# Neighbour weights in PSUM, key-query products on GpSimd, sums on VectorE, and key monomials over three chunks

## The chip, the core and the metric

The kernel runs on one core of a Trainium2 chip. The core has a matrix engine (TensorE, PE in the profile, with its weight loads shown as PEld), a vector engine (VectorE, DVE), a scalar engine (ScalarE, ACT), a general engine (GpSimd, POOL) and a queue engine that mostly starts transfers (SyncE, SP). Each works through its own instructions in order and waits for the others through semaphores. Data lies in SBUF (128 partitions) or in PSUM, where TensorE writes its results. The metric is the device time of one execution in microseconds.

## The reference

Four graph layers act on a table x of 2708 nodes by 128 features, with one 2708 x 2708 matrix `adj` of which some 0.15% of the entries, and the diagonal, differ from zero:

```python
h = relu(layernorm(x)); x = x + laplacian(adj) @ (h @ W + b)             # layer 0
h = relu(layernorm(x)); x = x + attention(h)                             # layer 1
h = relu(layernorm(x)); x = x + relu(batchnorm(adj.T @ h / deg ...))     # layer 2
h = relu(layernorm(x)); x = x + gated_sum(h, adj)                        # layer 3

# layer 1: d = 128 groups of 8 values, n = 2708
q = (x @ Wq.T).reshape(d, n, 8);  k, v alike
a = softmax(einsum('dnh,dmh->dnm', q, k) * d ** -0.5 + 2 * adj, axis=2)
out = einsum('dnm,dmh->dnh', a, v).reshape(n, 8 * d) @ Wo.T
```

Layer 1 takes most of the time. It is 128 attentions over all 2708 nodes, with 8 values per query and key.

## The kernel before

**How layer 1 is computed.** The kernel never forms the 2708 x 2708 logits. With no adjacency term, exp(q.k) is replaced by a polynomial in the 8 values of q and k, so that the sum over all keys becomes a small matrix of moments. The adjacency term is then put in exactly, for those pairs only where `adj` isn't zero (the neighbours), by adding exp(q.k)(exp(2 adj) - 1) times the value. The two parts are summed and divided by the summed weight (the ninth column of the values).

**The loop over d.** For each of the 128 d's, the 2708 nodes are 22 tiles of up to 128 rows, in six chunks of at most four tiles. The pieces of one d are:

- `keys(d)`: GpSimd makes the monomials of the keys (`bk` and `fk`, 12 products, all recorded at line 1010 as `mul_g` is the recording line). `with_values` makes `y`, low monomials times values, on GpSimd as well, in two halves.
- `moments`: TensorE multiplies `fk` by `y` and sums into `m_ps` (line 1048). `weighted` scales that into `mw` on VectorE (line 1058).
- `queries(d)`: VectorE makes the monomials of the queries (`fq`, line 1007).
- `turn(d, c)`: TensorE transposes `fq` of one chunk into `f_ps` (line 1074), and ScalarE copies it to `fT` (line 1076).
- `evaluate(d, c)`: TensorE multiplies `fT` by `mw` into `g_ps` (line 1086). VectorE multiplies by the low monomials (`z`, line 1094) and sums (`o_raw`, line 1100).

The loop is written out by hand, in what is called a manual schedule, so the order of the calls in the program is the order in each engine's queue. In each chunk it issues `keys(d + 2)` if the chunk is the first, `weighted` if it is the last, `evaluate(d, c)`, three steps of `queries(d + 1)`, `turn` for the next chunk, some of the `moments(d + 1)`, one half of `with_values(d + 2)` in the third and the last chunk, and one step of `prepare`, which loads the q, k and v of a later group of four d's.

**The work beside the loop.** After these calls every chunk takes PACE = 1.45 steps of a generator `first`, which is in turn: a search of `adj` for the neighbours together with gathers by node (`search`, `by_node`), then sorting the nodes by their number of neighbours (`in_order`), then `from_neighbours`. When it is used up, the chunk instead takes up to three steps of a second list, `beside`: `normalise(g)` for each of 32 groups of d's and `project_out` for each of 22 row tiles. What is left of `beside` is stepped through after the loop.

**`from_neighbours`.** The sorted nodes lie in 22 tiles with room for 16, 9, 8, ... 2 neighbours each (`ROOM`), 121 neighbour slots in all. For each slot b, GpSimd's queue loads the keys and values of the neighbours by an indirect transfer (`c_kv`, line 825, 1.05 MB). Then `logits(b)` multiplies keys by queries (`c_z`, line 840, VectorE), yields a step and sums over the 8 values (`c_c`, line 844, VectorE). `weigh(b)` takes the exponential and scales it on ScalarE. `values(b - 1)`, which is called between the two, first copies the previous slot's weights to the ninth column of `c_v` on ScalarE, then multiplies values by weights (line 870, VectorE), yields twice, and adds the product to the tile's sum `c_acc` (line 879, GpSimd). The first slot of a tile writes its product to `c_acc` directly, so 99 of the 121 have a sum. When a tile is finished, its sum is scattered to `more_n`. The weights `c_c` are tiles of 128 x 128 in SBUF, from a rotating pool.

**`normalise` and `project_out`.** `normalise(g)` loads the group's `o_raw` and `more_n`, adds them on GpSimd (`r_raw`, line 930), and on VectorE takes the reciprocal (`r_rs`, line 932) and the product (`r_on`), which is stored. `project_out(t)` loads a row tile and multiplies it by Wo (`l_o`, line 505, TensorE, into the pool `ps_t` of two buffers that `turn` also uses), and VectorE adds the result to `x_sb` (line 508).

**After the loop.** A guard reduces bounds of the data to two counts in `flag`, `once` and `heads`. Three loops over these counts recompute attention in full where the polynomial would not be accurate enough; for this data the counts are zero, and the loops are skipped. Then layer 2 loads its weights, takes `norm_relu`, makes 1/deg and spreads it over the partitions through 22 small products (`d_ps` into `diB`), and multiplies `h` by `adj` (`pg`), for which each tile of `adj` is loaded into `a2` from a pool of four buffers. Layer 3 follows.

Of the kernel before, what the change touches and what calls it, by code (L numbers as in the profile page):

```python
# [16 lines left out]
P = 128  # L17
BK = 512
# [31 lines left out]
def gnn4_kernel(  # L50
# [75 lines left out]
    few = keep.tile([P, 1], FP, name="few")  # L126

# [388 lines left out]
    with ExitStack() as ph:  # L516
# [8 lines left out]
        ps_t = ph.enter_context(tc.tile_pool(name="l1_pst", bufs=2, space=PSUM))  # L525
        ps_m = ph.enter_context(tc.tile_pool(name="l1_psm", bufs=1, space=PSUM))
        ps_g = ph.enter_context(tc.tile_pool(name="l1_psg", bufs=2, space=PSUM))
        ps_q = ph.enter_context(tc.tile_pool(name="l1_psq", bufs=1, space=PSUM))

# [272 lines left out]
        def from_neighbours():  # L802
# [6 lines left out]
            qs, kvs, cs, accs = {}, {}, {}, {}  # L809
            done = []  # L810
# [23 lines left out]
            def logits(b):  # L834
                t, s0, w = todo[b]
                sz = rows[t][1]
                cs[b] = sm.tile([P, S, C], FP, name="c_c")
                for e in range(w):
                    z = tm.tile([P, C, HEAD], FP, name="c_z", tag="tmp")
                    nc.vector.tensor_tensor(  # L840
                        z[:sz], kvs[b][:sz, e, :, 0], qs[t][:sz], ALU.mult
                    )
                    yield
# [14 lines left out]
            def values(b):  # L858
# [6 lines left out]
                for e in range(w):  # L865
# [11 lines left out]
                    yield  # L877
                    if s0 + e:
                        nc.gpsimd.tensor_tensor(acc[:sz], acc[:sz], z[:sz], ALU.add)  # L879
# [118 lines left out]
        PACE = 1.45  # L998
# [16 lines left out]
        def keys(d):  # L1015

            k = got[d // GRP][0][:, d % GRP, :, k_at]
            fks[d] = fp.tile([P, NT, F_ALL], FP, name="fk")
            run(features(mul_g, k, bks[d % 2], fks[d]))
# [86 lines left out]
        with tc.manual_schedule():  # L1106
# [4 lines left out]
            keys(0)  # L1111
# [3 lines left out]
            keys(1)  # L1115
# [10 lines left out]
            for d in range(D):  # L1126
                asked = queries(d + 1) if d + 1 < D else iter(())
                for c in range(NCH):
                    if d + 2 < D and c == 0:
                        while len(got) <= (d + 2) // GRP:  # L1130
                            run(soon.pop(0))
                        keys(d + 2)
# [29 lines left out]
                if (d + 2) % GRP == 0 and (d + 2) // GRP + 1 < NG:  # L1162
                    soon.append(prepare((d + 2) // GRP + 1, got))
            while beside or under_way:
# [4 lines left out]
    with ExitStack() as ph:  # L1169
        gp = ph.enter_context(tc.tile_pool(name="l1g", bufs=1))  # L1170
        gw = ph.enter_context(tc.tile_pool(name="l1g_w", bufs=2))
        g_l = ph.enter_context(tc.tile_pool(name="l1g_l", bufs=1, space=PSUM))
        g_t = ph.enter_context(tc.tile_pool(name="l1g_t", bufs=1, space=PSUM))
        g_o = ph.enter_context(tc.tile_pool(name="l1g_o", bufs=1, space=PSUM))
        q_f = dram.tile([N, P, HEAD], FP, name="q_f")
        k_f = dram.tile([N, P, HEAD], FP, name="k_f")
        v_f = dram.tile([N, P, VW], FP, name="v_f")
        o_f = dram.tile([N, P, HEAD], FP, name="o_f")

        nc.vector.memset(top, 0.0)
        p2 = gp.tile([C, 2], FP, name="p2")
        for e in range(2):
            pt = g_t.tile([P, BK], FP, name="g_tr", tag="tr")
            nc.tensor.transpose(pt[:C, :P], most2[:, e], ident)
# [414 lines left out]
```

## Time and profile before

| What | Value |
|---|---|
| Time, median of 3 runs | 4456.89 us (4449.6 to 4462.39) |
| The profiled execution's own time | 4452.14 us |
| Its span in the trace | 4450.3 us |
| Busy: PE, DVE, ACT, POOL | 3230.9, 3549.0, 1101.9, 2789.4 us |
| First `z` to last `o_raw` of the loop | 470.2 us to 3921 us |
| First to last neighbour product `c_z` | 1318.7 us to 3300.7 us |
| TensorE clock granted, mean | 0.842 |

The span runs from the first to the last record of the core, and the device time is about 2 us more. A group's row gives line, engine, operation, output and inputs, shape and count, then the busy time in us and the mean of one in ns, then the idle time of the engine just ahead of these instructions and what ended most of it. A tile's row gives the minimum, median and maximum of one in ns, and when the first began and the last ended. Busy time of an engine that waits inside an instruction[...] counts as busy.

### The profile page before, as it was taken

Reading aid. Unit: us, or ns where it says so; the run is one execution under the profiler, and the core shown is the slowest. Engines: PE = TensorE matmul, PEld = TensorE weight load, DVE = VectorE, ACT = ScalarE, POOL = GpSimd, SP = SyncE. Lnnn points to the kernel's source line nnn. Section 1 sums busy time; section 2 is a strip of 40 time slices with the busy share of each in tenths; the row PEclk is TensorE's granted clock in tenths of the full one; section 3 lists DMA queues with packets and bytes.
Section 4 is the critical chain, followed back from the end, with each engine's and each line's share of the span. In section 5 each row is a group of like instructions: output and inputs, shape, how many; then the busy total and the mean of one; then the engine's idle time right before and its main releaser. Section 6 shows DMA issues by size and latency. Waiting matters only on the chain. (4 is left out here: it accounts for less than half of the span.)

```text
span 4450.3 us, 49671 instructions
## 1 busy us (share of the span) xinstructions
PE 3230.9 (73%) x17298; PEld 2879.4 (65%) x17298; DVE 3549.0 (80%) x4852; ACT 1101.9 (25%) x2497; POOL 2789.4 (63%) x2384
## 2 busy tenths in 40 slices
PE   7986788888857777776777766767767788949434
PEld 5953677788756666666666656667657787834223
DVE  5988899987849989999988999999977777840322
ACT  4246233333312222222222222222221111210110
POOL 0001766677767887887878777678876666700266
PEclk9988889899978888888888888888888899979565
DMA  4637344367412222222222222222324454035232
GB/s 181 225 143 304 101 108 123 98 140 178 110 54 80 84 79 90 90 91 81 90 90 91 81 76 96 82 94 97 104 70 105 112 113 96 23 103 203 75 86 70
DMA packets 402006, 480.25 MB, mean 108 GB/s; under 512 B 290672, under 2 KB 322098, under 8 KB 376916
## 3 DMA queue, kind: packets, MB, share of 16 engines
q1 hardware_dynamic: 370140, 308.03, 24.1%
q0 software_dynamic: 31600, 168.86, 11.5%
q8 instruction: 144, 2.36, 0.2%
q14 instruction: 122, 1.00, 0.1%
HBM read 363.13 MB, written 113.67 MB: 107 GB/s over the span
## 5 line engine op out<-in xcount | busy, mean ns | idle before, releaser
L1086 PE MATMUL g_ps<-mw,fT 128*128 128x189 f32 x5632 | 1227.8, 366 | 699.1 <-DVE mw L1058 397.8
L1086 PEld LDWEIGHTS g_ps<-mw,fT 128*128 128x128 f32 x5632 | 1043.2, 215 | 781.0 <-issue 521.9
L1010 POOL TENSOR_TENSOR y<-bk,raw 128x2079 f32<-128x2079 f32 x256 | 976.2, 3814 | 516.1 <-PE m_ps L1048 478.3
L1048 PE MATMUL m_ps<-y,fk 128*128 128x189 f32 (+1 forms) x5632 | 1101.7, 340 | 21.3 <-POOL y L1010 21.3
L1048 PEld LDWEIGHTS m_ps<-y,fk 128*128 128x128 f32 (+1 forms) x5632 | 963.5, 203 | 50.5 <-issue 28.7
L1076 ACT COPY fT<-f_ps 128x512 f32<-128x512 f32 (+1 forms) x768 | 422.7, 550 | 1962.1 <-PE f_ps L1074 1960.1
L1094 DVE TENSOR_TENSOR z<-g_ps,bq 128x756 f32<-128x756 f32 (+1 forms) x768 | 669.4, 872 | 202.4 <-PE g_ps L1086 201.7
L1100 DVE TENSOR_REDUCE o_raw<-z 128x36 f32<-128x756 f32 (+1 forms) x768 | 672.5, 876 | 26.3
L1074 PE MATMUL f_ps<-ident,fq 128*128 128x128 f32 x2816 | 490.3, 299 | 38.9 <-DVE fq L1007 36.2
L1010 POOL TENSOR_TENSOR fk<-bk,raw 128x528 f32<-128x528 f32 (+1 forms) x512 | 508.2, 1021 | 0.0
L1074 PEld LDWEIGHTS f_ps<-ident,fq 128*128 128x128 f32 x2816 | 400.5, 157 | 75.7 <-issue 31.5
L840 DVE TENSOR_TENSOR c_z<-c_kv,c_q 128x1024 f32<-128x1024 f32 (+1 forms) x121 | 419.5, 3467 | 10.6 <-DMA c_kv<-kv_n,srt 10.6
L879 POOL TENSOR_TENSOR c_acc<-c_acc,c_v 128x1152 f32<-128x1152 f32 (+1 forms) x99 | 262.1, 2647 | 165.6 <-DVE c_v L870 119.1
L1010 POOL TENSOR_TENSOR fk<-raw,bk 128x352 f32<-128x352 f32 (+1 forms) x512 | 317.7, 649 | 0.0
L1007 DVE TENSOR_TENSOR fq<-bq,q_ps 128x528 f32<-128x528 f32 (+1 forms) x512 | 288.0, 604 | 0.0
L870 DVE TENSOR_TENSOR c_v<-c_kv,c_c 128x1024 f32<-128x1024 f32 (+1 forms) x99 | 244.5, 2470 | 1.3 <-POOL c_acc L879 1.3
L465 POOL MEMSET qkv<- 128x512 f32 x6 | 6.3, 1083 | 374.8 <-PE l_o L350 255.4
L1010 POOL TENSOR_TENSOR bk<-raw 128x88 f32<-128x88 f32 (+1 forms) x512 | 216.7, 454 | 33.4 <-DMA raw<-qkv_c 32.9
L1420 POOL DMA_INDIRECT g<-gate_d,srt x121 | 122.6, 1013 | 107.7 <-issue 107.7
L825 POOL DMA_INDIRECT c_kv<-kv_n,srt x121 | 137.3, 1135 | 60.2 <-DVE c_acc L870 37.5
L1007 DVE TENSOR_TENSOR fq<-q_ps,bq 128x352 f32<-128x352 f32 (+1 forms) x512 | 171.7, 377 | 0.0
L505 PE MATMUL l_o<-woT,o_cr 128*128 128x128 f32 (+1 forms) x352 | 95.8, 421 | 81.2 <-DMA o_cr<-o_c 40.2
(284 smaller groups left out, 3502.7 us busy)
## 6 DMA issues: line engine op xcount, KB each, us to landing
a_nat<-in_adj_dram SPq DMA_DIRECT2D x32, 1354.0 KB
qkv_c<-qkv SPq DMA_DIRECT2D x5, 6400.0 KB
a<-in_adj_dram SPq DMA_DIRECT2D x21, 1354.0 KB
kv_n<-n_kv SPq DMA_DIRECT2D x32, 672.0 KB
an<-in_adj_dram SPq DMA_DIRECT2D x15, 1354.0 KB
o_g<-o_raw SPq DMA_DIRECT2D x32, 396.0 KB
r_raw<-o_g SPq DMA_DIRECT2D x32, 396.0 KB
r_more<-more_n SPq DMA_DIRECT2D x32, 396.0 KB
```

The lines of the kernel that those rows point to most:

```text
L825: nc.gpsimd.indirect_dma_start(out=kvs[b][:sz, e].rearrange("p c e k -> p (c e k)"), out_offset=None, in_=kv_n.rearrange("n c k -> n (c k) ...
L840: nc.vector.tensor_tensor(z[:sz], kvs[b][:sz, e, :, 0], qs[t][:sz], ALU.mult)
L870: nc.vector.tensor_tensor(z[:sz, :, :HEAD], kv[:sz, e, :, 1], c[:sz, e, :, None].to_broadcast([sz, C, HEAD]), ALU.mult,)
L879: nc.gpsimd.tensor_tensor(acc[:sz], acc[:sz], z[:sz], ALU.add)
L1007: nc.vector.tensor_tensor(o, x, y, ALU.mult)
L1010: nc.gpsimd.tensor_tensor(o, x, y, ALU.mult)
L1048: nc.tensor.matmul(pms[d][:, : B_ALL * VW], fks[d][:sz, t], ys[d, h][:sz, m].rearrange("p k b -> p (k b)"), start=t == 0, stop=t == NT - 1,)
L1074: nc.tensor.transpose(pt[:, m], fqs[d][:, t0 + m], ident)
L1076: nc.scalar.copy(fts[d, c][:, :n], pt[:, :n])
L1086: nc.tensor.matmul(pg[:, m, : B_ALL * VW], ft[:, m], mws[d].rearrange("p k b -> p (k b)"), start=True, stop=True,)
L1094: nc.vector.tensor_tensor(z[:, :n], pg[:, :n, : B_ALL * VW].rearrange("p t (k b) -> p t k b", k=VW), bqs[d % 2][:, t0 : t0 + n, None, :B_A ...
L1100: nc.vector.reduce_sum(ros[g][:, t0 : t0 + n, i], z[:, :n], axis=AX.X,)
```

## The change

1. `logits`: the product `c_z` of keys and queries is issued on GpSimd, and there are two yields instead of one ahead of its reduction on VectorE.
2. The weights `c_c` are no longer SBUF tiles. Two slots alternate in one PSUM tile, `c_two`, from a new pool `ps_c` of one bank. To make room, `ps_t` has one buffer where it had two.
3. `values`: the sum into `c_acc` is issued on VectorE, one yield after `c_v`. A first slot now has one yield and the others two; before, every slot had two.
4. PACE is 1.58 instead of 1.45.
5. `keys(d + 2)` is a generator. Five of its products are issued in the first chunk, five in the second and the last two in the third.
6. The guard stands ahead of the leftover steps of `beside`, takes its buffers from the loop's pools, and `flag` is kept in a longer-lived pool.
7. Layer 2's weights, biases, `diB` and the loads of the first four `adj` tiles stand ahead of the three loops of the fallback, which moved inside layer 2. `norm_relu` stays after them.

```diff
-        ps_t = ph.enter_context(tc.tile_pool(name="l1_pst", bufs=2, space=PSUM))
+        ps_t = ph.enter_context(tc.tile_pool(name="l1_pst", bufs=1, space=PSUM))
...
+        ps_c = ph.enter_context(tc.tile_pool(name="l1_psc", bufs=1, space=PSUM))
...
+            c_two = ps_c.tile([P, 2, S, C], FP, name="c_c")
...
-                cs[b] = sm.tile([P, S, C], FP, name="c_c")
+                cs[b] = c_two[:, b % 2]
                 for e in range(w):
                     z = tm.tile([P, C, HEAD], FP, name="c_z", tag="tmp")
-                    nc.vector.tensor_tensor(
+                    nc.gpsimd.tensor_tensor(
                         z[:sz], kvs[b][:sz, e, :, 0], qs[t][:sz], ALU.mult
                     )
+                    yield
                     yield
                     nc.vector.reduce_sum(cs[b][:sz, e], z[:sz], axis=AX.X)
...
                     yield
-                    yield
                     if s0 + e:
-                        nc.gpsimd.tensor_tensor(acc[:sz], acc[:sz], z[:sz], ALU.add)
+                        nc.vector.tensor_tensor(acc[:sz], acc[:sz], z[:sz], ALU.add)
+                        yield
...
-        PACE = 1.45
+        PACE = 1.58
...
-            run(features(mul_g, k, bks[d % 2], fks[d]))
+            yield from features(mul_g, k, bks[d % 2], fks[d])
...
-                        keys(d + 2)
+                        keyed = keys(d + 2)
+                    if d + 2 < D:
+                        for _ in range(5 if c < 2 else NCH * 3):
+                            next(keyed, None)
...
+            nc.vector.memset(top, 0.0)
+            p2 = sm.tile([C, 2], FP, name="p2")
...
             while beside or under_way:
                 if not step(n, NG):
                     n += 1
-        nc.vector.memset(top, 0.0)
-        p2 = gp.tile([C, 2], FP, name="p2")
...
+        with tc.tile_pool(name="l2_ps0", bufs=2, space=PSUM) as ps:
+            wnT = transposed(lp, wk_pool, ps, wn2, "wnT")
...
+            for t, (r0, sz) in enumerate(rows):
+                dg = lp.tile([P, P], FP, name="dg", tag="dg", bufs=2)
+                nc.vector.tensor_scalar_mul(dg[:sz, :sz], ident[:sz, :sz], di[:sz, t : t + 1])
+                pd = ps.tile([P, BK], FP, name="d_ps", tag="tr")
+                nc.tensor.matmul(pd[:, :sz], ones[:sz], dg[:sz, :sz], start=True, stop=True)
+                nc.scalar.copy(diB[:, r0 : r0 + sz], pd[:, :sz])
+        for t in range(min(4, NT)):
+            rows_of_adj2(t)
```

## The prediction

> **What bounds the kernel now.** I read the page first, then busy time by stage, then the tiles of the neighbour code, then a timeline. The page has the engines' busy time and the groups that the change touches.
>
> ```profile
> PE 3230.9 (73%) x17298; PEld 2879.4 (65%) x17298; DVE 3549.0 (80%) x4852; ACT 1101.9 (25%) x2497; POOL 2789.4 (63%) x2384
> ...
> L840 DVE TENSOR_TENSOR c_z<-c_kv,c_q 128x1024 f32<-128x1024 f32 (+1 forms) x121 | 419.5, 3467 | 10.6 <-DMA c_kv<-kv_n,srt 10.6
> L879 POOL TENSOR_TENSOR c_acc<-c_acc,c_v 128x1152 f32<-128x1152 f32 (+1 forms) x99 | 262.1, 2647 | 165.6 <-DVE c_v L870 119.1
> ...
> L870 DVE TENSOR_TENSOR c_v<-c_kv,c_c 128x1024 f32<-128x1024 f32 (+1 forms) x99 | 244.5, 2470 | 1.3 <-POOL c_acc L879 1.3
> ```
>
> No engine is full over the span, so I cut it into stages by the tiles' first and last times: the search, the gathers by node, the sorting in order, the neighbours, the normalisation, the rest of the loop, the tail, layers 2 and 3. Columns after window and length: busy PE, weight load, DVE, ACT, POOL; clock; DMA share; GB/s.
>
> ```profile
> 470.00:910.00 440.00, 349.44 (x1993) 327.02 (x1991) 419.24 (x558) 140.17 (x263) 287.20 (x268) 0.88 0.41 104
> 910.00:1210.00 300.00, 271.38 (x1659) 254.80 (x1660) 244.53 (x413) 116.36 (x227) 227.04 (x206) 0.97 0.65 151
> ...
> 1318.00:3305.00 1987.00, 1410.41 (x7605) 1321.85 (x7606) 1871.96 (x2180) 453.86 (x1149) 1576.43 (x1229) 0.84 0.26 87
> 3305.00:3770.00 465.00, 371.76 (x2028) 351.31 (x2027) 340.22 (x549) 79.97 (x187) 315.21 (x264) 0.88 0.46 105
> 3770.00:3921.00 151.00, 137.05 (x849) 128.67 (x847) 123.21 (x203) 34.42 (x77) 94.75 (x83) 0.98 0.10 24
> ```
>
> The neighbours' 1987 us are 45% of the span, and VectorE is busy for 1872 of them (94%), GpSimd for 79%, PE for 71%. So VectorE sets the pace there. Yet its neighbour products take longer than they need (minimum/median/maximum ns):
>
> ```profile
> L840 DVE TENSOR_TENSOR c_z<-c_kv,c_q x121: 1215/3453/14609, 1318.7 to 3300.7; 128x1024 f32<-128x1024 f32 x119, 20x1024 f32<-20x1024 f32 x2
> L870 DVE TENSOR_TENSOR c_v<-c_kv,c_c x99: 1212/1653/8760, 1343.7 to 3322.6; 128x1024 f32<-128x1024 f32 x98, 20x1024 f32<-20x1024 f32 x1
> L844 DVE TENSOR_REDUCE c_c<-c_z x121: 1197/1210/1223, 1322.2 to 3305.5; 128x128 f32<-128x1024 f32 x119, 20x128 f32<-20x1024 f32 x2
> L1094 DVE TENSOR_TENSOR z<-g_ps,bq x768: 725/932/969, 470.2 to 3920.6; 128x756 f32<-128x756 f32 x128, 128x567 f32<-128x567 f32 x64
> ```
>
> Both products read two SBUF operands and range widely; the reduction (one operand) and z (one operand in PSUM) don't. The timeline (start, duration) shows why:
>
> ```profile
> 1668.04 3.78 POOL L1010 TENSOR_TENSOR y<-bk,raw 128x2079 f32<-128x2079 f32 x1
> 1669.19 3.72 DVE L840 TENSOR_TENSOR c_z<-c_kv,c_q 128x1024 f32<-128x1024 f32 x1
> 1673.02 1.22 DVE L844 TENSOR_REDUCE c_c<-c_z 128x128 f32<-128x1024 f32 x1
> ```
>
> c_z ends 1.1 us after y does (1671.82), that is, one undisturbed product later: it had stood behind GpSimd's instruction.
>
> [...]
>
> **The change, part by part.** The loop has 768 chunks, each with one z. The built order says how many lie before the first neighbour's reduction, between the first and the last, and after: 213/412/143 before, 196/441/131 after. A neighbour takes more steps (704 in all against 605), so there are .274 per chunk instead of .294.
>
> Neighbour stage, VectorE per chunk. Before, 1872 less the neighbours' own instructions (419.5 + 121×1.21 + 244.5 + 47.0 for the 21 first-neighbour products = 857.5) is 1014 over 412 chunks, 2.46 us, unchanged. After, per neighbour: c_z 0 here; reduction 1.21; c_v 1.22, because its weight comes from PSUM and it no longer contends (saving 1.25 on 99 of them); the sum c_acc, now on VectorE with two SBUF inputs, in .818 of the neighbours (99/121): 1.36 if free, up to 3.9 if it waits as c_z did (c_z's mean wait of 2.25 plus 1.36 is 3.6). Taken 3.3, since GpSimd is about as busy as before. Bank waits: in the built order 40 of 121 reductions stand directly ahead of the previous neighbour's c_v, while ScalarE's weight copy stands between them; I take 0.55 us for the copy and hand-offs, .18 per neighbour (0 to .3). Lateness of GpSimd: .3 per neighbour (0 to 2.5). Sum 1.21+1.22+.818×3.3+.18+.3 = 5.61; ×.274 = 1.54. With 2.46 and the .28 of other idle per chunk as before ((1987-1872)/412), 4.28 us per chunk, ×441 = 1887: **-100**. Ends: 3.96 per chunk (1746, -241), where the sum hardly waits (VectorE then needs 3.7) and GpSimd, below, is the next bound; and 4.45 (1962, -25) with the sum at 3.9 and the bank at .3, the mishap R3 apart.
>
> GpSimd per chunk. Before, 1576.4 - 262.1 (sums) - 137.3 (loads' issue) = 1177/412 = 2.86. After, 2.86 + .274×(1.14 + 2.4 for c_z, 1024×2.3 ns) = 3.83, which is 89% of 4.28. So it is the second bound, close behind. PE's moment products wait for its y, and the c_kv loads are issued from its queue.
>
> Where the product moves, GpSimd's queue matters. A c_z may stand behind a y (3.8 us) or key monomials (12 products, 8.5 us, in one block before; now 5, 5 and 2). Its reduction is programmed two steps later, 2/1.58 chunks × 4.28 = 5.4 us. If it is late, everything of VectorE stands behind the reduction, z too, and then PE with both g_ps buffers full. In the trace GpSimd runs ahead: the sums start a median 0.14 us, mean 2.3, and in one of ten 8.3 after their c_v, though they are programmed some 6.6 us later; lateness beyond 5.4 us is then rare, hence .3.
>
> Fewer chunks ahead: the search ends at chunk 99 instead of 107; VectorE, 95% busy there, saves 8×2.46 = 20. The gathers save 8 chunks at PE's 3.3 (its cycle is 18 to 20 us per six chunks): 26. Sorting, which waits for DMA, and the same work in fewer chunks: +2. Together **-44**.
>
> Fewer chunks after: 12×2.6 (between VectorE's 2.46 and PE's 3.2) = **-31**; the normalisations themselves take the same number of steps.
>
> ps_t from two buffers to one (its place goes to the weights): a transpose then waits for ScalarE's 0.55 us copy of the one before, and l_o for VectorE's x_sb add. It is hidden while VectorE bounds (PE is 71% busy), but not in 3305 to 3921, where PE is 80 to 91%: **+30** (0 to 60).
>
> Key monomials spread: y's products no longer wait for 8.5 us of monomials, worth something in the PE-bound stages, -20 (0 to -40); but normalisation's r_raw products move later in GpSimd's queue, +10 (VectorE's r_rs waits 34.8 us for r_raw there now). **-10**.
>
> Tail: the guard (4.5 us of VectorE) goes ahead of the last normalisation, which waits for r_more's landing: -4.5, hidden there. One loop skip (about 3 us of 9.3) comes while the tail still works: -3. The 22 small products for diB move ahead of the skips, serial over three engines: +12, less 5 to 9 of PE in layer 2 where they lay before; the adjacency loads start sooner, but layer 2's product is PE-bound (4.54 us per tile), so this earns nothing. **+2** (-8 to +15).
>
> Sum: -100 -44 -31 +30 -10 +2 = -153. The profiled run took 4452.1 (span 4450.3, 2 us around it), so 4299; the median of the runs shown is 4.8 higher, so **4305**.
>
> **Rivals.** R1, the port wait nearly vanishes. The sum now follows c_v on VectorE and may meet short GpSimd monomials rather than y; at 3.96 us per chunk a further -141: 4165. Against it: GpSimd's busy share hardly falls. Chance .17. R2, GpSimd becomes the bound: busy 3.83 plus the waits it keeps (y for PE's m_ps, 131 us in this stage now, .32 per chunk; c_z for the landing or for buffers) gives 4.4 to 4.6 per chunk, 4350 to 4440. For it: 89% leaves little room. Chance .17. R3, slower: c_z reaches the front of GpSimd's queue too late and VectorE stands at the reduction. From 4305, a mean extra wait w costs 121×w; from w = 1.25 us it cancels the gain, and at 2.5 (half a y and some monomials each time) the time is 4305 + 300 = 4605, less what the wait takes from the sum's port wait, some 60: 4545. Against it: GpSimd runs ahead now, and it gives up 262 us of sums for 290 of products (2.4×121) that are spread over 29 more chunks. Chance .08. R4, the weight in PSUM does not free c_v: +1.25×99 = 124, so 4430. Against it: z's tight durations. Chance .04.
>
> **How the numbers follow.** Likeliest .54, 4235 to 4365 by its own terms. Runs of this kernel differ by about 0.3% (13 us), so the border of faster is 4444. R1 and R2's lower part are inside 4195 to 4420, which leaves out R3, R4 and the far tails, about .2. Faster: .54 + .17 + .15 + .02 = .88; same: .02 + .01 = .03 from R2 and R4; slower: R3 and some of R4, .09.
>
> **What would show it.** Right: in the neighbour stage about 4.3 us per chunk, c_v tight at 1.22 to 1.25 us, c_acc on VectorE 3 us in the mean and as wide as c_z was, c_z on GpSimd 2.3 to 2.5, GpSimd near 89%, little wait of the reduction for c_z (under 40 us in all), a ScalarE wait around c_c of some 20 us; the stage begins some 44 us sooner. Wrong: waits of the reduction for GpSimd of over 100 us (R3); waits on y or c_kv that grow while VectorE falls under 85% (R2); c_acc under 2 us (R1); c_v still over 1.6 us (R4); PE waits for ScalarE's copy beyond 60 us after the stage (ps_t).

## The result, and the profile after

The changed kernel takes 4428.92 us in the median (14 runs, 4415.62 to 4445.41), the kernel before 4455.6 us beside it (14 runs). The ratio is 0.9944, with a 95% interval from 0.9922 to 0.9966. So it is faster by 25 us (0.6%), about one sixth of the 150 that were forecast, and it lies above the range of 4195 to 4420. The profiled execution has a span of 4420.4 us, 30 less than the one of before.

The stages show where the forecast was lost. Lengths are taken between the same instructions in both traces: the loop's first z, the first c_z, the end of the last reduction into c_c, the loop's last z, the end.

| Stage | Before, us (chunks) | After, us (chunks) | Difference | Forecast |
|---|---|---|---|---|
| Search, gathers, sorting | 848 (213) | 817 (196) | -31 | -44 |
| Neighbours | 1988 (412) | 1984 (441) | -4 | -100 |
| Rest of the loop | 614 (143) | 614 (131) | 0 | -11 |
| From the last z to the end | 530 | 536 | +6 | +2 |

Such lengths vary by themselves. The changed kernel and seven of the kernels below have the same code, at PACE 1.58, from the neighbours to the last z; the rest of the loop takes 614 to 637 us in them. The run with the old tail, which has the changed kernel's neighbour code, takes 1993 us for that stage instead of 1984.

The page of the changed kernel, with busy time and share per engine, and then the groups that were moved (busy us, mean ns, idle time ahead):

```profile
PE 3259.3 (74%) x17298; PEld 2894.7 (65%) x17298; DVE 3374.6 (76%) x4830; ACT 1092.1 (25%) x2497; POOL 2792.6 (63%) x2406
...
L882 DVE TENSOR_TENSOR c_acc<-c_acc,c_v 128x1152 f32<-128x1152 f32 (+1 forms) x99 | 379.5, 3834 | 1.4
...
L843 POOL TENSOR_TENSOR c_z<-c_kv,c_q 128x1024 f32<-128x1024 f32 (+1 forms) x121 | 285.9, 2363 | 2.1 <-DMA c_kv<-kv_n,srt 0.7
```

VectorE lost 174 us of busy time (3549.0 to 3374.6), GpSimd kept its own (2789.4 to 2792.6). Yet the span fell by 30 only. The same by stage, for the neighbours and the rest of the loop (columns as before: window, length, then busy PE, weight load, DVE, ACT, POOL):

```profile
1287.00:3271.00 1984.00, 1479.80 (x8138) 1390.04 (x8139) 1770.68 (x2285) 467.61 (x1206) 1662.27 (x1333) 0.86 0.26 89
3271.00:3885.00 614.00, 492.28 (x2647) 458.77 (x2645) 424.26 (x690) 103.90 (x240) 372.92 (x307) 0.88 0.36 84
```

In the neighbour stage VectorE is busy for 1771 us (1872 before) and idle for 213 (115 before). So of its work 101 us went, although 29 more chunks lie in the stage, and 98 us came back as idle time. The tiles tell which work remained (minimum/median/maximum ns):

```profile
L843 POOL TENSOR_TENSOR c_z<-c_kv,c_q x121: 2307/2341/3452, 1287.2 to 3255.9; 128x1024 f32<-128x1024 f32 x119, 20x1024 f32<-20x1024 f32 x2
L874 DVE TENSOR_TENSOR c_v<-c_kv,c_c x99: 1195/1216/1223, 1315.2 to 3275.3; 128x1024 f32<-128x1024 f32 x98, 20x1024 f32<-20x1024 f32 x1
L882 DVE TENSOR_TENSOR c_acc<-c_acc,c_v x99: 1347/2754/12153, 1318.2 to 3276.6; 128x1152 f32<-128x1152 f32 x98, 20x1152 f32<-20x1152 f32 x1
```

c_v, with its weight in PSUM, is now as tight as z was: every one takes 1.2 us. The sum has inherited the wide spread of c_z: 1.35 us where it is free, 12.2 at worst, 3.83 in the mean. VectorE's waits in the neighbour stage tell where it stood idle: the instruction, what it waited for, us in all, times, longest. The two longest before the change, and then those after it:

```profile
DVE c_acc L870 <- DMA more_n<-c_acc,srt: 47.5, 11, 12.2
DVE z L1094 <- PE g_ps L1086: 44.1, 47, 1.8
```

```profile
DVE z L1098 <- PE g_ps L1090: 82.4, 75, 3.3
DVE c_acc L874 <- ACT c_acc L873: 65.5, 19, 9.3
DVE c_c L848 <- POOL c_z L843: 34.2, 23, 5.9
DVE c_v L874 <- ACT c_v L873: 15.5, 32, 0.8
```

The line of c_acc after the change is put down to ScalarE's copy into a fresh c_acc; that copy itself had waited for the scatter of the tile before (105.9 us in all, 17 times). Ahead of the reduction and of c_v, VectorE's idle time before the change was 3 and 1 us.

What a long sum is waiting for shows in the timeline of one that took 9.0 us (start, duration; GpSimd, then VectorE):

```profile
1384.70 3.83 POOL L1014 TENSOR_TENSOR fk<-bk,raw 128x528 f32<-128x528 f32 x4
1388.51 3.75 POOL L1014 TENSOR_TENSOR y<-bk,raw 128x2079 f32<-128x2079 f32 x1
1392.41 1.91 POOL L828 DMA_INDIRECT c_kv<-kv_n,srt  x1 [0.16 <-issue]
...
1384.48 9.00 DVE L882 TENSOR_TENSOR c_acc<-c_acc,c_v 128x1152 f32<-128x1152 f32 x1
```

The forecast had read c_z's wait as one for the GpSimd instruction in progress. This sum waited longer than that: through four more key products and a y, which follow one another without a gap, and ran when GpSimd paused by 0.16 us ahead of a load.

### The profile page after: what moved, and what is told of

Its sections match the earlier page's. It is cut to its first block, busy times and chain, and to the rows that moved or that the text cites. A ratio compares the mean times of both kernels' runs of the same rounds, so it can differ in the third digit from the quotient of the medians.

```text
span 4420.4 us, 49434 instructions
## 1 busy us (share of the span) xinstructions
PE 3259.3 (74%) x17298; PEld 2894.7 (65%) x17298; DVE 3374.6 (76%) x4830; ACT 1092.1 (25%) x2497; POOL 2792.6 (63%) x2406
## 5 line engine op out<-in xcount | busy, mean ns | idle before, releaser
L1052 PE MATMUL m_ps<-y,fk 128*128 128x189 f32 (+1 forms) x5632 | 1118.5, 344 | 34.6 <-POOL y L1014 34.6
L1052 PEld LDWEIGHTS m_ps<-y,fk 128*128 128x128 f32 (+1 forms) x5632 | 977.9, 206 | 64.2 <-POOL y L1014 35.3
L882 DVE TENSOR_TENSOR c_acc<-c_acc,c_v 128x1152 f32<-128x1152 f32 (+1 forms) x99 | 379.5, 3834 | 1.4
L843 POOL TENSOR_TENSOR c_z<-c_kv,c_q 128x1024 f32<-128x1024 f32 (+1 forms) x121 | 285.9, 2363 | 2.1 <-DMA c_kv<-kv_n,srt 0.7
L828 POOL DMA_INDIRECT c_kv<-kv_n,srt x121 | 167.2, 1382 | 128.2 <-DVE c_v L874 50.8
L1014 POOL TENSOR_TENSOR bk<-raw 128x88 f32<-128x88 f32 (+1 forms) x512 | 195.7, 412 | 33.8 <-DMA raw<-qkv_c 33.5
L848 DVE TENSOR_REDUCE c_c<-c_z 128x128 f32<-128x1024 f32 (+1 forms) x121 | 147.7, 1221 | 34.3 <-POOL c_z L843 34.2
L506 PE MATMUL l_o<-woT,o_cr 128*128 128x128 f32 (+1 forms) x352 | 107.2, 442 | 82.4 <-DVE x_sb L509 56.5
```

Source lines behind the costliest of these rows:

```text
L828: nc.gpsimd.indirect_dma_start(out=kvs[b][:sz, e].rearrange("p c e k -> p (c e k)"), out_offset=None, in_=kv_n.rearrange("n c k -> n (c k) ...
L843: nc.gpsimd.tensor_tensor(z[:sz], kvs[b][:sz, e, :, 0], qs[t][:sz], ALU.mult)
L848: nc.vector.reduce_sum(cs[b][:sz, e], z[:sz], axis=AX.X)
L882: nc.vector.tensor_tensor(acc[:sz], acc[:sz], z[:sz], ALU.add)
L1014: nc.gpsimd.tensor_tensor(o, x, y, ALU.mult)
L1052: nc.tensor.matmul(pms[d][:, : B_ALL * VW], fks[d][:sz, t], ys[d, h][:sz, m].rearrange("p k b -> p (k b)"), start=t == 0, stop=t == NT - 1,)
```

## The experiments

What the forecast and the expectations call the wait for the port is here a group's busy time less its count times what one takes when free (1.216 us for a product, 1.353 for a sum). That a port which VectorE and GpSimd share is behind it was my reading and is not shown. The traces show durations: with both operands in SBUF, c_z took 1215 to 14609 ns before the change and the sum 1347 to 12153 after it; with one of them in PSUM, c_v took 1195 to 1223 beside a GpSimd that was busy for 1662 of the 1984 us. In the neighbour stage before the change these port waits are 419.5 - 121×1.216 = 272 us in c_z, 240.0 - 98×1.216 = 121 in c_v and 21 in the first products, 414 in all; after it, 376.3 - 98×1.353 = 244, all in the sum. Every run below was timed in five rounds against the kernel before; its ratio has an interval of about 0.0025 to each side (11 us) unless one is given. The column "us" compares it with the changed kernel, as (ratio - 0.9944)×4440; such a difference is good to some 15 us.

| Run | Ratio | us | Neighbour stage, us | VectorE busy / idle there | Port waits |
|---|---|---|---|---|---|
| changed kernel | 0.9944 | 0 | 1984 | 1771 / 213 | sum 244 |
| sum with one SBUF input | 0.9808 | -60 | 1906 | 1699 / 207 | product 231 |
| sum with one input in PSUM | 0.9438 | -225 | 1757 | 1517 / 240 | none |
| engines swapped back | 1.0062 | +52 | 2005 | 1824 / 181 | c_z 287 |
| weights in SBUF, one ps_t | 1.0176 | +103 | 2088 | 1884 / 204 | c_v 171, sum 183 |
| weights in SBUF, two ps_t | 1.0081 | +61 | 2112 | 1938 / 174 | c_v 199, sum 206 |
| keys in one block | 1.0091 | +65 | 2015 | 1742 / 273 | sum 213 |
| PACE 1.45 | 0.9785 | -71 | 2040 (480 chunks) | 1815 / 225 | sum 190 |
| copy ahead of the reduction | 0.9843 | -45 | 1933 | 1737 / 196 | sum 213 |

**Is VectorE still the bound?** Two edits of the sum, each of one instruction, and each leaves the earlier neighbours out:

```diff
-                        nc.vector.tensor_tensor(acc[:sz], acc[:sz], z[:sz], ALU.add)
+                        nc.vector.tensor_scalar_mul(acc[:sz], z[:sz], 1.0)
```

> The changed kernel, with VectorE's sum of c_acc and c_v replaced by a product of c_v with 1.0, so that the instruction reads one SBUF operand; the earlier neighbours' sum is left out of the result. V (VectorE still sets the pace of the neighbour stage, and the sum's wait for the port, (3834 - 1357) x 99 = 245 us, is what ate the gain): the instruction takes 1.4 us at most, the stage loses 200 to 245 us of its 1984, the time falls to 4190 to 4240. P (another engine or wait bounds the stage now, so VectorE's time is no longer worth its length): the time falls by less than 90 us, to 4340 or more, and VectorE's idle time grows by over 150 us.

It gave 4354.78 us, 0.9808. By its time that is P's case, but VectorE's idle time did not grow (207 us): the instruction still waited.

```profile
L882 DVE TENSOR_SCALAR c_acc<-c_v x99: 748/1799/11549, 1315.9 to 3195.4; 128x1152 f32<-128x1152 f32 x98, 20x1152 f32<-20x1152 f32 x1
```

It is fast where it is free (748 ns, where the sum of as many elements takes 1347), and as wide as the sum otherwise; its mean in the stage is 3108 ns, so it waits 2.36 us where the sum waits 2.49. The reduction too reads one SBUF operand, and it doesn't wait inside itself (1197 to 1223 ns before the change). I had counted operands only, and their number does not tell the two apart; what does is not shown. What was saved, 72 us of VectorE's busy time, came off the stage in full (78). The second edit takes operands like those of c_v's own product, which is tight: one in SBUF, one in PSUM (lines joined):

```diff
-                        nc.vector.tensor_tensor(acc[:sz], acc[:sz], z[:sz], ALU.add)
+                        nc.vector.tensor_tensor(
+                            acc[:sz, :, :HEAD], z[:sz, :, :HEAD],
+                            c[:sz, e, :, None].to_broadcast([sz, C, HEAD]), ALU.mult)
```

> The changed kernel with the sum replaced by a product of c_v and the weights in PSUM (1024 elements, one SBUF operand and one in PSUM, as c_v's own product is); the earlier neighbours' sum is left out of the result. This takes away the port's wait that the product with 1.0 had kept (3.1 us in the mean). V (VectorE's length sets the neighbour stage): the instruction takes 1.22 us, the stage loses (3840 - 1220) x 98 = 257 us less what GpSimd, 84% busy, and TensorE give back as new waits, so 150 to 250 us, and the time falls to 0.94 to 0.963 of the kernel before. P (another engine is next at once): the stage loses under 110 us, idle time of VectorE rises above 350 us, 0.97 or more.

It gave 4196.26 us, 0.9438 (0.9413 to 0.9463), at the good end of V. Its tile and its neighbour stage:

```profile
L882 DVE TENSOR_TENSOR c_acc<-c_v,c_c x99: 1204/1215/1224, 1321.4 to 3055.8; 128x1024 f32<-128x1024 f32 x98, 20x1024 f32<-20x1024 f32 x1
...
1290.00:3048.00 1758.00, 1420.28 (x8143) 1335.83 (x8144) 1517.38 (x2285) 465.80 (x1205) 1577.46 (x1331) 0.90 0.30 100
```

VectorE's busy time fell by 254 us, the stage by 227, to 3.98 us per chunk, and there GpSimd is the busiest engine (90%). So at 4.50 us per chunk neither GpSimd nor TensorE was the bound: VectorE's length was, with its waits in place.

**What does the swap earn?** In the changed kernel, with each instruction at its new place:

```diff
-                    nc.gpsimd.tensor_tensor(
+                    nc.vector.tensor_tensor(
                         z[:sz], kvs[b][:sz, e, :, 0], qs[t][:sz], ALU.mult
...
-                        nc.vector.tensor_tensor(acc[:sz], acc[:sz], z[:sz], ALU.add)
+                        nc.gpsimd.tensor_tensor(acc[:sz], acc[:sz], z[:sz], ALU.add)
```

> The changed kernel with both engines swapped back: c_z on VectorE, the sum on GpSimd, each at its new place in the program. Everything else (weights in PSUM, one ps_t buffer, pace, key monomials, tail) stays. S (the swap earns nothing, since the port wait goes with whichever two-SBUF-input instruction VectorE has): c_z 3.3 to 3.6 us on VectorE (+410), the sum's 380 off it, the time within 30 us of the changed kernel, 4400 to 4460. O (the swap is what earned the gain, the weights in PSUM nothing): 4460 or more. H (the swap itself costs, by putting VectorE behind GpSimd at the reduction): 4330 to 4400.

4464.02 us, 1.0062: just at O's number, 52 us slower, though O's reason (the weights earn nothing) does not hold, as the runs on the weights show. In the neighbour stage it costs 21 us only: VectorE is busy 53 longer, 43 of them port waits (287 in c_z for 244 in the sum), and idle 32 less. After it the loop takes 637 us instead of 614, which is within what the same code varies by, so where the rest of the 52 lies is open. VectorE's wait for g_ps is 45 us here and 82 in the changed kernel. It is 44 to 49 in every profiled kernel with c_z on VectorE and 67 to 104 in every one with c_z on GpSimd; why the product's place should make TensorE late is not shown. The same swap alone, on the kernel before (with its yields, PACE 1.45):

> The kernel before with the swap alone: c_z on GpSimd, the sum on VectorE, with the yields of the change, PACE 1.45, weights in SBUF, keys in one block. E (the swap gains by itself, as its undoing says): 0.975 to 0.99. I (without the spread keys c_z comes late, and c_v takes the waits that c_z had): waits of the reduction for c_z over 60 us, c_v's waits over 200 us, 0.995 to 1.02.

4470.56 us, 1.0099 (1.0078 to 1.012): slower by 44, inside theory I's range, with both of its waits a little under the size that it named:

```profile
L871 DVE TENSOR_TENSOR c_v<-c_kv,c_c x99: 1202/1748/11214, 1355.0 to 3527.0; 128x1024 f32<-128x1024 f32 x98, 20x1024 f32<-20x1024 f32 x1
L879 DVE TENSOR_TENSOR c_acc<-c_acc,c_v x99: 1335/2065/11768, 1358.1 to 3529.8; 128x1152 f32<-128x1152 f32 x98, 20x1152 f32<-20x1152 f32 x1
```

Now c_v waits 165 us and the sum 150, and the reduction stands 59 us for c_z. VectorE has two waiting instructions per neighbour, as it had before.

**The PSUM edit.** In the changed kernel, first the weights alone go back (their PSUM pool goes too), then the second ps_t buffer as well:

```diff
-                cs[b] = c_two[:, b % 2]
+                cs[b] = sm.tile([P, S, C], FP, name="c_c")
```

> The changed kernel with the weights c_c back in rotating SBUF tiles, and still one ps_t buffer. W (c_v has to wait for the port again, 1.25 us each in 99, and the bank's waits go): +124 - 16 = about +108 in VectorE's stage, 4500 to 4550. B (the bank's waits cost about as much as the port): 4410 to 4450.

> The same, with two ps_t buffers as before the change, so the whole of the edit on PSUM is undone. Against the run with one buffer: T (the single buffer makes TensorE late, f_ps behind v_sum in the neighbour stage, l_o behind x_sb after it): 50 to 90 us faster, with VectorE's waits for g_ps and l_o back at 44 and 30 us in these stages. N (it only costs in the normalisation stage): 20 to 40 us faster. If it falls below the changed kernel's time, the edit on PSUM as a whole was a loss.

4516.64 us (1.0176) and 4481.16 us (1.0081). The weights in PSUM are worth 103 us, as W said: without them c_v has 171 us of port waits and the sum 61 less. The single ps_t buffer costs 42 by the ratios (35 by the medians), which is N, so the whole edit on PSUM is worth 61. VectorE's waits for g_ps in the neighbour stage are 82 with one buffer and 67 with two, and the stage is no shorter with two (2112 for 2088, in a profiled run 19 us above the median of its runs); after the stage the loop takes 614 us against 585, and x_sb shows where (the groups of the two runs in that stretch, one buffer first; idle time ahead is the last number):

```profile
L509 DVE TENSOR_TENSOR x_sb<-x_sb,l_o 128x128 f32<-128x128 f32 x72 | 20.5, 285 | 62.1 <-PE l_o L506 61.8
```

```profile
L509 DVE TENSOR_TENSOR x_sb<-x_sb,l_o 128x128 f32<-128x128 f32 x72 | 20.5, 284 | 29.5 <-PE l_o L506 28.2
```

The edit alone on the kernel before:

> The kernel before with the edit on PSUM alone: weights c_c in one PSUM tile of two slots, one ps_t buffer. E (the edit pays by itself, as its undoing on the changed kernel says): c_v 1.22 us, VectorE's waits in c_v and first products (142 us) gone, some 42 us lost to the single buffer, 0.975 to 0.987 of the kernel before. I (c_z takes over c_v's waits, since a VectorE that is ahead meets GpSimd sooner, or the bank's order costs as much): c_z's waits rise from 272 to over 350 us, 0.99 to 1.005.

4393.26 us, 0.9921: 35 us faster, less than E. The number is in I's range, but not for I's reason: c_z did not take the waits over, it waited less (234 us for 272). VectorE's idle time took them over:

```profile
DVE c_acc L872 <- ACT c_acc L871: 124.6, 19, 12.6
DVE z L1096 <- PE g_ps L1088: 45.6, 58, 2.1
DVE c_v L872 <- ACT c_v L871: 19.0, 32, 2.1
```

The stage lost 180 us of port waits (414 to 234) and 71 in length, because the wait of a tile's first product for the last tile's scatter went from 48 to 125 us, and 19 us went to the wait of c_v for ScalarE's copy.

**The key products.** With all twelve in the first chunk again:

```diff
-                        for _ in range(5 if c < 2 else NCH * 3):
+                        for _ in range(NCH * 3):
```

> The changed kernel with all twelve key products issued in the first chunk again. L (the spreading makes fk late for the moments or delays c_z and normalisation): faster than the changed kernel by 20 to 50 us, 0.983 to 0.990 of the kernel before. G (it helps c_z reach GpSimd in time): slower by 10 to 50 us, with VectorE's wait for c_z up from 34 us to over 60; 0.997 to 1.006.

> The kernel before with the key products spread over three chunks alone. E (spreading pays by itself, y comes sooner and the runs on GpSimd are shorter): 0.983 to 0.993 of the kernel before. I (it pays only with c_z behind the key products in GpSimd's queue): 0.995 to 1.01.

4481.26 us (1.0091), 65 slower: G in its sign and more than its size. The reduction's wait for c_z rose to 75.8 us (35 times), and after the stage the loop takes 659 us, 22 to 45 more than in the runs with the spread keys. Alone on the kernel before the spreading gives 4391.63 us, 0.9932: 30 us, at E's edge, so it pays by itself, and about twice as much when c_z and the sum are where the change put them.

**The pace.** PACE 1.45, 1.33, and 1.58 up to chunk 196 with 1.45 from there:

> The changed kernel with 1.45 steps per chunk as before. The neighbour stage then has 704/1.45 = 486 chunks, and begins some 17 chunks later. If a chunk costs VectorE 2.5 us in the neighbour stage and saves as much elsewhere (M), the time is within 25 us of the changed kernel; if the chunks that move from the PE-bound end into the stage save more there than they cost (F), it is 30 to 60 us slower or, with fewer normalisation steps per chunk colliding, as much faster.

> The changed kernel with PACE 1.33, one step further than the run with 1.45: 529 chunks in the neighbour stage and next to none after it, so all normalisation falls behind the loop. C (a chunk is cheaper inside the neighbour stage, some 1.4 us at the margin, than after it, some 2.8): faster again than at 1.45, by 0 to 50 us, until what is left behind the loop is no longer covered: 0.965 to 0.98 of the kernel before. U (what helped at 1.45 was the way that the steps fall on the six chunks of a d, or the sum's shorter waits there): about the changed kernel's time or worse, 0.985 to 1.01.

> The changed kernel with 1.58 steps per chunk up to chunk 196, where the neighbours begin, and 1.45 from there on. C (chunks have a price by the stage they lie in): the search and sorting as at 1.58 (817 us), the neighbour stage as at 1.45 (2040), and the 18 chunks that the search gives up come after it at 2.8 us each, so -22 + 50 = +28 us against PACE 1.45 throughout, 0.983 to 0.987 of the kernel before. U (it is how the steps fall on the six chunks of a d): the neighbour stage is not within 30 us of 2040.

| | Changed, 1.58 | 1.45 | 1.33 | 1.58, then 1.45 |
|---|---|---|---|---|
| Ratio | 0.9944 | 0.9785 | 0.9935 | 0.9826 (0.9793 to 0.9859) |
| Up to the neighbours, us (chunks) | 817 (196) | 839 (214) | 901 (233) | 822 (196) |
| Neighbours | 1984 (441) | 2040 (480) | 2162 (524) | 2040 (481) |
| Rest of the loop | 614 (131) | 379 (74) | 37 (11) | 465 (91) |
| From the last z to the end | 536 | 613 | 836 | 552 |

1.45 gained 71 us, more than either of its theories; I had not asked for a gain of that size. The stages of that run:

```profile
470.00:1310.00 840.00, 676.53 (x3976) 631.97 (x3975) 716.98 (x1062) 272.56 (x525) 582.48 (x561) 0.91 0.46 114
1310.00:3350.00 2040.00, 1563.28 (x8892) 1468.40 (x8890) 1814.94 (x2458) 498.76 (x1279) 1764.66 (x1426) 0.88 0.26 88
3350.00:3729.00 379.00, 287.30 (x1483) 267.81 (x1483) 255.60 (x398) 58.11 (x134) 207.30 (x167) 0.84 0.40 92
```

The 18 chunks more ahead of the neighbours cost 22 us (1.2 each), the 39 more among them 56 (1.4 each, since the sum's waits fall from 244 to 190 where neighbours are thinner), the 57 fewer after them save 235 (4.1 each), and 77 come back behind the loop, where the left-over normalisation has nothing beside it. That sums to -80 between two profiles; the ratios give -71. The run with two paces has the stage lengths that C forecast, 822 and 2040, and its ratio is 0.9826, just under C's range of 0.983 to 0.987; its interval does not separate it from 1.45 throughout. At 1.33 the time is in U's range, but the stages tell C's story: little is left to save after the neighbours, and what falls behind the loop costs 300 us more than at 1.58. So the runs fit a pace that acts through the prices of the stages, and the sign that U named, a neighbour stage away from 2040, did not come.

**The order of ScalarE's copy.** The copy, product and sum of the last neighbour ahead of the next reduction (the first of two places):

```diff
                     yield
+                    store()
+                    if b:
+                        yield from values(b - 1)
                     yield
                     nc.vector.reduce_sum(cs[b][:sz, e], z[:sz], axis=AX.X)
```

> The changed kernel with the order of one neighbour's calls turned: the previous neighbour's weight copy, product and sum are issued between c_z and its reduction instead of after it. So the copy on ScalarE no longer stands behind the reduction that is in the same bank, and c_z has two steps more. K (the bank's order makes ScalarE late: its copy waits 164 us for the reduction, fT is queued behind it, then g_ps and z): VectorE's waits for c_z, the copy and g_ps (34, 15 and 82 us) fall by 60 to 100 in all, the time by 40 to 90 us against the changed kernel, 0.975 to 0.986 of the kernel before. N (ScalarE has room, the copy's wait costs nothing, and z waits for other reasons): within 20 us of the changed kernel, 0.990 to 0.999.

4368.4 us, 0.9843: 45 faster, K's size, but not on K's way. The waits for c_z and for the copy fell from 34 and 15 us to 5 and 1, the port waits by 31; the wait for g_ps stayed (81), and that for the scatter rose to 94. So K's path, from the copy over fT to z, was not what made z late.

With PACE 1.45 and an earlier scatter in addition:

> The changed kernel with three edits that the runs and the trace point to: the copy, product and sum issued ahead of the next reduction; PACE 1.45; and the scatter of a finished c_acc issued ahead of the next c_z instead of after its reduction (VectorE waits 66 us for it at first slots). If they add up: -45 -71 -40 against the changed kernel, so 0.955 to 0.967 of the kernel before. If the first two take the same slack (VectorE's waits): 0.968 to 0.980.

4363.11 us, 0.9827: above both ranges, and no faster than PACE 1.45 alone. The sum's waits are 238 us against 190 there, and the first products' wait for the scatter is 83: issuing the scatter earlier did not help, and these gains do not add.

**A break for the sum, and the tail.** The load of c_kv moved to just ahead of the sum, three slots ahead (the first of two places); and, in another run, the end of the program put back as it was:

```diff
+                    if b + 3 < len(todo):
+                        load(b + 3)
                     if s0 + e:
                         nc.vector.tensor_tensor(acc[:sz], acc[:sz], z[:sz], ALU.add)
```

> The changed kernel with each c_kv load issued just ahead of a sum in the program (three slots ahead) instead of one step after it. GpSimd then waits at the load for VectorE's c_v whenever it runs ahead[...]. R (a waiting sum is let through only at a break in GpSimd's run of instructions, and the break before a load is the usual one): the sum's mean falls from 3.83 us to under 2.6 us, VectorE's neighbour stage by 100 us or more if GpSimd, 84% busy, can give the time up, the time to 0.96 to 0.98 of the kernel before. Q (GpSimd's time is what is short, so its waiting at the load is paid back as late y and c_z): the sum falls as said, but VectorE's waits for g_ps and c_z rise by as much, 0.985 to 1.005.

> The changed kernel with the guard, the layer-2 constants and the first adjacency loads at their places of before the change. D (as in the forecast: hidden guard and one skip against serial small products): within 15 us of the changed kernel, 0.991 to 0.998 of the kernel before, the stretch from the loop's last z to the end within 15 us. A (the moved work is worth more, since it runs while the last normalisation waits for its loads): 15 to 30 us slower than the changed kernel.

The load gave 4403.78 us, 0.9919: no difference that can be told. The sum's waits fell to 213 us, not to the 120 that R asked for, and c_z's lateness rose from 34 to 52. R is not confirmed: moving the load does not give the sum its break, and that a break lets the sum through stays a reading of traces, counted in the last section. The tail back gave 4419.38 us, 0.9953 (0.9937 to 0.9969), 4 us from the changed kernel: D. Its stretch from the last z to the end is 515 us, and 511 to 518 in eight runs with the new tail at PACE 1.58, so that stretch varies by more than the edit moves it (530 and 536 in the two main profiles).

**A version that takes the wait out of the sum.** The half of the weights' bank that is free holds 32 features of a product, so c_v is made and added in four pieces (the added lines, joined and shortened):

```diff
+                    for j, (c0, n) in enumerate(_cuts(C, CUT)):       # CUT = 32
+                        nc.vector.tensor_tensor(
+                            piece[:sz, :n], kv[:sz, e, c0 : c0 + n, 1],
+                            c[:sz, e, c0 : c0 + n, None].to_broadcast([sz, n, HEAD]), ALU.mult)
+                        nc.vector.tensor_tensor(
+                            acc[:sz, c0 : c0 + n, :HEAD], acc[:sz, c0 : c0 + n, :HEAD],
+                            piece[:sz, :n], ALU.add)
+                        if j == 1:
+                            yield
+                    nc.vector.tensor_tensor(acc[:sz, :, HEAD], acc[:sz, :, HEAD], c[:sz, e], ALU.add)
```

> The changed kernel with PACE 1.45, and c_v made and added in four pieces of 32 features, each of which lies in the free half of the weights' PSUM bank, so no instruction of VectorE in the neighbour code reads two SBUF operands; the weights' column is added straight from PSUM. Nothing is left out. Eight instructions of 256 elements at about 0.4 us (from z, 756 elements in 0.93, and c_v, 1024 in 1.22) and one of 128 at 0.28 make 3.5 us per neighbour instead of 1.22 + 1.35 + 1.94 of waiting (PACE 1.45 has 190 us of it in 98): the stage loses some 100 us if it goes by VectorE's length, 0.95 to 0.963 of the kernel before. If the pieces wait for one another or ScalarE for the bank, 0.97 or more.

4285.82 us, 0.9678 (0.9659 to 0.9698): clearly faster than PACE 1.45 alone (0.9785), short of its range by 20 us. Its piecewise sums no longer vary:

```profile
L890 DVE TENSOR_TENSOR c_acc<-c_acc,c_c x396: 407/420/424, 1336.4 to 3288.6; 128x256 f32<-128x256 f32 x196, 20x256 f32<-20x256 f32 x2
```

The nine instructions take 168.5 + 166.5 + 37.3 = 372 us, 3.8 per neighbour instead of 3.5, and the wait for g_ps rose to 104. VectorE is busy 80 us less in the stage than at PACE 1.45 (1735 for 1815), and the stage is 67 shorter. This version also drops ScalarE's 99 copies into c_v and takes no more of the buffers that c_v shared with c_z; what these do by themselves was not tried. The waits for the scatter (70) stayed, and went with one more line:

```diff
-                    accs[t] = lp.tile([P, C, VW], FP, name="c_acc", tag="n_kv")
+                    accs[t] = lp.tile([P, C, VW], FP, name="c_acc", tag=("n_kv", "c_acc2")[t % 2])
```

> The sum in pieces at PACE 1.45, with c_acc in two places that alternate by tile, so that a first product does not wait for the last tile's scatter. If that wait (70 us of VectorE's idle time) is worth its length: 0.950 to 0.957 of the kernel before. If the time goes into the waits for g_ps: 0.963 to 0.969.

4206.04 us, 0.9467 (0.9443 to 0.949), 237 us faster than the kernel before and past its range. The neighbour stage is 1899 us for 480 chunks:

```profile
1310.00:3209.00 1899.00, 1536.37 (x8879) 1441.55 (x8878) 1733.23 (x3145) 472.09 (x1183) 1681.02 (x1425) 0.91 0.28 94
```

VectorE is as busy there as it was with one c_acc (1735), and the stage 74 us shorter. Here VectorE's wait for the scatter was worth its full length.

## Why the prediction was wrong

**The neighbour stage, -100.** This is the step that failed; it measured -4. Its direction (VectorE sets the pace, c_v tight, the sum wide) held, and three of its terms were mis-sized: the sum's wait, the other idle time and, slightly, the base per chunk. By the forecast's own sum VectorE is busy 441×(2.46 + .274×(1.21 + 1.22 + .818×3.3)) = 1705 us and idle 181. It was busy 1771 and idle 213, which is 98 more. Even the forecast's bad end for the stage, -25 with the sum at 3.9, was too good.

- "Taken 3.3" for the sum: it measured 3.84, (3.84 - 3.3)×98 = 53 us more. The free sum, put at 1.36, took 1.35. The wait that c_z had, carried over, gave 3.6 by the forecast's own sum, and going below it had no reason: "GpSimd is about as busy as before" speaks for 3.6. That is 29 of the 53. For the other 24, a waiting instruction stood behind several GpSimd instructions that followed without a gap: 67 of 99 sums waited by over 0.25 us, through 2.6 GpSimd instructions in the mean; before, 89 of 121 c_z, through 2.4. The change does lengthen GpSimd's stretches of arithmetic without a gap over 0.1 us, from 6.3 to 7.6 us in the mean of the neighbour stage. But at PACE 1.45 they are 9.0 us and the sums wait less (190 us for 244), and with the keys in one block they are as long as here and the sums wait 213. So their length alone does not set the wait; what does is open. The 13 us by which VectorE's busy time is longer besides are mostly its base per chunk, 2.50 instead of 2.46.
- ".28 of other idle per chunk as before": the waits for g_ps rose from 44 to 82 us and those for the scatter from 48 to 66. The chunks grew by 7%, these by 61%; idle time other than for the bank and c_z came to .37 per chunk, 41 us more than forecast. It was carried over as fixed, with no range and no reason. The run with the edit on PSUM alone shows the wait for the scatter growing directly (48 to 125): VectorE reaches a tile's first product sooner, and the scatter of the tile before is not done. The forecast should have named it, as the row was in the profile. Why g_ps comes late is not shown.
- The bank (.18 per neighbour, 22 us; as measured, c_v's wait for ScalarE's copy) and GpSimd's lateness (.3, 36 us) measured 15 and 34: right.

**The pace.** This is the second cost that it missed. The forecast took the chunk counts from the built order and credited -44 and -31 for fewer chunks ahead and after. It never priced PACE by itself, and the runs show that PACE 1.58 costs 71 us against 1.45, with the other edits in place. The credit ahead measured -31. Behind the neighbours, -31 for the chunks was paid back by ps_t's +30: with two ps_t buffers that stretch is 585 us, 29 less than before, and with one it is 614. So both terms fit in size, as far as a stretch that varies by 23 us can tell, and that the whole stretch came out at 0 is no proof of them, since the keys are worth 22 to 45 us there too. What was missing is that the denser work leaves the normalisation in the costlier chunks (4.1 us each) rather than behind the loop.

**Key monomials, -10.** Worth 30 us alone and 65 in the changed kernel. It was mis-sized; and with its gain booked in the stages that TensorE bounds, I missed that c_z waits behind the block there (34 to 76 us).

**The tail, +2.** Its measured effect is 4 us within an uncertainty of about 15.

**The rivals.** R1 would have needed a sum under 2 us: no. R2 gave the right time per chunk (4.4 to 4.6, measured 4.50) and a range that holds the measured time (4350 to 4440), but by luck, for its reason was wrong: with the sum's wait removed the same work of GpSimd fits into 3.98. R3's wait measured 34 us in all, no more than the forecast's own 36; it needed 151 beyond that to cancel the gain. R4 is excluded by c_v at 1195 to 1223 ns. The swap, which I had costed as the main gain, loses 44 us alone and gains only in company: alone -35 (PSUM), -30 (keys) and +44 (swap, at PACE 1.45) make -21, and all three together at 1.45 make -95 (tail included). The stage lengths of the swap alone and of PACE 1.45, both with 480 chunks, differ by 2199 - 2040 = 159 us: c_v's waits of 165 + 17 are gone, the sum waits 40 more, and idle time falls by 19.

## What to carry to other kernels

When an instruction whose duration is wide moves off an engine, ask what instruction that engine has left with the same operand form, here two SBUF operands, and book for it the wait that the profile shows until there is a reason for less: 2.25 us in c_z before the change, 2.49 in the sum after it. The wait went with the operand form here, not with the work, and a PSUM operand removed it (1195 to 1223 ns for c_v), even in four pieces that cost 3.8 us instead of 2.6. When a bound engine gets faster, look up what it already waits for, here a scatter that one more buffer hides: such rows need not grow with the chunks (61% for 7% here). And give a knob like PACE a price of its own before it is turned together with other edits.

## What the runs showed of the hardware that I had not expected

- A VectorE sum of 1152 elements from two SBUF operands took 1.35 us when free and up to 12.2 us, and in the traces its wait mostly ends where GpSimd's stream of instructions breaks. The wait lasted through several of GpSimd's instructions, nine in the longest. Inside the 67 waits of over 0.25 us, GpSimd went from one instruction to the next 110 times, at a gap of -0.03 us in the median (records overlap) and never over 0.1. Of the waits' ends 51 lie at a gap over 0.1 us (0.16 in the median of all) and 16 between two adjoining instructions. In c_z's 89 waits before the change, none of 124 such steps had a gap over 0.1 us, and 30 waits ended between adjoining instructions. So no wait lasted through a break of over 0.1 us, and about a quarter and a third of the waits ended without one.
- A product by a constant with a single SBUF operand waited about as long as a sum with two, 2.36 against 2.49 us in the mean; when free it took 748 ns, where the sum took 1347.
- Four pieces of 256 elements through a PSUM bank cost 0.426 us (product) and 0.420 us (sum) each in the mean, the sums without spread (407 to 424 ns). With two c_acc the sums took 407 to 424 ns again, beside a GpSimd that was busy for 1681 of the stage's 1899 us.
